# One more pair's softmax denominators on VectorE, and multiplies and token sums on GpSimd, in a two-layer convolution and attention kernel

## The chip, the cores and the metric

The kernel runs on one core of one Trainium2 chip, as one launch. The metric is the device time of one execution in microseconds (us). A core has TensorE (PE, matrix products into PSUM), VectorE (DVE), ScalarE (ACT), GpSimd (POOL) and SyncE (SP), each with an instruction stream of its own, taken in order; SP here issues the DMAs. All data are float32.

## The reference

Eight images of 768 channels and 32 x 32 = 1024 tokens go through two layers, each of which adds to its input:

```python
x = x + attention(group_norm(x))          # layer 0
x = x + correlation_conv(group_norm(x))   # layer 1

def attention(x):                          # 12 heads of 64
    q, k, v = split(x_flat @ W_qkv.T)
    var_v, var_k = var(v, axis=-1, ddof=1), var(k, axis=-1, ddof=1)   # one number per token
    attn = softmax(var_v @ var_k.T * 64 ** -0.5)
    return (attn @ v) @ W_proj.T + b_proj

def correlation_conv(f):
    n = f / max(norm(f, axis=channels), 1e-12)
    corr = [sum(shifted(n, r, c) * n, axis=channels) for r, c in 28 offsets]
    return conv_w @ concat(f, corr) + conv_b                          # 1 x 1
```

The scores are an outer product of two vectors, so that no score matrix product is needed: an exponential of one row, scaled per partition, gives a block of the softmax's numerator.

## The kernel before, in words

**Products.** The three large products (keys and values, projection, convolution) are made by a scheme of seven block products in place of eight; it needs sums of operand blocks (`TokenSums`, L1030, for projection and convolution; `make_sums`, L595, on GpSimd for keys and values) and adds the seven results up in PSUM banks x, y and z (`Banks`, L340 on; both halves of a product are issued by `halves`, L333 to L337). A unit is one such block product: 1.93 us by the plan for keys and values, 2.58 for the wide ones. After a unit, VectorE (in part ScalarE) takes the bank to SBUF. The next unit that adds to that bank waits for this. The token sums are t1, t2, a third that is written over the input, and t4, three instructions of 128x512 each; their names in the profile end in f for the convolution, in o for the projection.

**Attention.** An image has six pairs of heads. For a pair, `exponentials` (L733) makes on ScalarE two tiles ex of 128x1024 for each of eight steps; `products` (L757) multiplies them with the values on TensorE (av, L763). Four steps are run together. The denominators are had in one of two ways, by the table `SUMMED` (L47):

- a pair not in it makes them on ScalarE: `denominators` (L742), 16 further exponentials junk from the tiles bk, then an inverse on VectorE (invs), a transpose on TensorE (it, in `spread`, L870) and a DMA through memory (di) that spreads it over partitions as rd;
- a pair in it adds its ex tiles up on VectorE (acc, L775), 14 additions; then `sum_up` (L790) sums over the partitions by four matmuls of 32 columns (den, L797), ScalarE copies, and DMAs bring the sums to a narrow tile inv for the reciprocal and back as rd. The image's last pair (`sum_up_last`, L840) instead makes wide sums by L847 and four reciprocals of 128x256 (`invert`, L853), with no DMA.

`finish` (L885) multiplies the pair's result (tile v) by the inverses. The acc tiles and the bk tiles share two buffers; rd has one. Image 0 sums pairs 0, 3, 4 and 5; the others 3, 4 and 5.

**Correlation.** `Corr` (L1069) multiplies blocks of the normalised image, turned by GpSimd (turn, L1086), with the image (gr, L1101), takes windows (win) out through DRAM, and scales them (dd, m, rn on GpSimd in L1146, dn); `to_dram` transposes dn on TensorE (ct, L340) and a DMA gathers rows cs. The convolution adds cs by short products (L1008) to its banks.

**Order.** No engine is told when to start; the program's order is computed while it is built, with a model clock (`Clock`, L79). `later.after(us, job)` issues a job when the model clock has moved on by us; `after_dve` counts from the end of VectorE's modelled work; `ready` holds keys of what has been issued, and `act_work` queues ScalarE's. `work_off` chooses between four attention steps, a correlation product beside it and the next unit of the rest: the second half of keys and values, then the previous image's convolution. Then `project` makes the projection, and the next image's first half of keys and values follows. On the chip each engine takes its instructions in that order and waits by semaphores for data and buffers.

**Start.** Image 0 is loaded and its group norm made; meanwhile 36 products of the identity with itself run on TensorE (warm, L390). `Norm.means` and `Norm.spreads` (L476, L487) then put two small products on TensorE, pm and pv; GpSimd makes the power rstd, and the image is scaled (xn). L153 is the line of a helper through which every VectorE instruction goes, L215 that of ScalarE's copies.

Of the kernel before, what the change touches and what calls it, by code (L numbers as in the profile page):

```python
# [13 lines left out]
P = 128  # L14
# [32 lines left out]
SUMMED = ((0, 3, 4, 5), (3, 4, 5))  # L47
# [7 lines left out]
WARM = 36  # L55
# [103 lines left out]
def two_layers(ctx, tc, x, wkv, wproj, bproj, wconv, wcorr, bconv, out):  # L159
# [308 lines left out]
    class Norm:  # L468
# [239 lines left out]
    class Pair:  # L708
# [131 lines left out]
        def sum_up_last(self):  # L840
# [189 lines left out]
    class TokenSums:  # L1030


        def __init__(self, name, low, high, third=None):
            self.low, self.high = low, high
            self.name = name
            self.third = third or [a[:, HF:] for a in low]
# [4 lines left out]
        def first(self):  # L1041
            self.t1 = self.place(1)
            for k in range(JH):
                a = self.low[k]
                vector.tensor_tensor(self.t1[:, k, :], a[:, HF:], a[:, :HF], ALU.subtract)

        def second(self):
            self.t2 = self.place(2)
            for k in range(JH):
                vector.tensor_tensor(self.t2[:, k, :], self.high[k][:, HF:], self.t1[:, k, :], ALU.subtract)  # L1050

        def thirds(self):
            for k in range(JH):
                vector.tensor_tensor(self.third[k], self.high[k][:, HF:], self.low[k][:, HF:], ALU.subtract)

        def fourth(self):
            self.t4 = self.place(4)
            for k in range(JH):
                vector.tensor_tensor(self.t4[:, k, :], self.high[k][:, :HF], self.t2[:, k, :], ALU.subtract)
# [9 lines left out]
    class Corr:  # L1069
# [70 lines left out]
        def scale(self, hf, dd):  # L1140
# [7 lines left out]
            def columns():  # L1148
# [4 lines left out]
                later.after_dve(0.7, lambda: to_dram(dn))  # L1153
# [46 lines left out]
    class Conv:  # L1200


        def __init__(self, b, f, acc, after):
# [4 lines left out]
            self.sums = TokenSums(f"f{b}", [f[:, k, :] for k in range(JH)], [f[:, JH + k, :] for k in range(JH)])  # L1208
# [124 lines left out]
    def project(b, ots, held=None):  # L1333
# [35 lines left out]
        sums = TokenSums(f"o{b}", ots[:JH], ots[JH:])  # L1369
# [166 lines left out]
```

## Time and profile before

| What | Value |
|---|---|
| median of 3 runs | 2643.72 us (2642.43 to 2647.05) |
| the profiled execution, its own time | 2640.38 us |
| its span | 2638.7 us |
| granted TensorE clock, mean | 0.998 |
| ScalarE denominators (junk, L748) | 368, mean 1143 ns |
| what ends each (read of the sum) | 368, mean 187 ns |
| VectorE additions acc<-acc,ex and acc<-ex,ex | 300 of 1209 ns and 50 of 1215 ns |
| VectorE multiplies v<-v,rd and v<-v,acc | 40 of 1211 ns and 8 of 1223 ns |
| VectorE token sums (t1f, f, t2f, t4f; the o ones alike) | 128x512, 663 to 687 ns |
| GpSimd sums s, 128x384 | 256, 1003 to 1098 ns by line |
| rd loads from di, from den | 46, 34 of 256 KB |

In the profile an engine's row gives its busy time and its share of the span. Groups of instructions show the line, the engine, the operation, what is written and read (out<-in, buffer numbers left out), the shape and the count. The waits name who waited for whom, in us in total, times and the longest. The timeline gives start, duration, engine, line and operation, and in brackets the idle time of the engine in front of it with what ended it. A product of a whole tile is two records on TensorE; both halves of a unit run beside one another. Images are counted from 0; attention of image 3 runs from about 1003 us to 1192, its projection from about 1207.

### The profile page before, as it was taken

What the parts mean: (1) busy time and instruction counts of PE and PEld (TensorE: products, weight loads), DVE (VectorE), ACT (ScalarE), POOL (GpSimd) and SP (SyncE); (2) the same over time, 40 slices, a digit from 0 to 9 for tenths busy, and PEclk for the clock granted to TensorE, in tenths of its full rate; (3) what the DMA queues carried; (4) which work ended last, traced back from release to release, by engine and by line L of the source; (5) the groups of instructions that cost most, each with busy time, mean ns of one, the idle gap of its engine ahead of it and who ended that gap; (6) DMA issues with size and microseconds to landing.
All of it is one profiled execution on the core that took longest, in us unless ns stands there. A gap on an engine that the chain in (4) does not pass through costs nothing.

```text
span 2638.7 us, 40466 instructions
## 1 busy us (share of the span) xinstructions
PE 2610.0 (99%) x14766; PEld 1318.2 (50%) x14766; DVE 1604.3 (61%) x4110; ACT 1367.3 (52%) x1841; POOL 413.6 (16%) x444
## 2 busy tenths in 40 slices
PE   9999999999999999999999999999999999999999
PEld 4654566334763347633476334553357433575333
DVE  5858735685447853478534885357853587535864
ACT  1498078711598116980179701897018960199500
POOL 4320130003300033000430003300133001320000
PEclk9999999999999999999999999999999999999999
DMA  7774455455553545626556265562655626545333
GB/s 285 291 247 147 144 198 158 137 182 159 188 187 113 201 153 180 198 95 214 155 172 196 87 220 158 171 205 81 221 172 154 196 84 237 169 137 164 96 117 101
DMA packets 323392, 446.65 MB, mean 169 GB/s; under 512 B 59458, under 2 KB 245170, under 8 KB 323194
## 3 DMA queue, kind: packets, MB, share of 16 engines
q1 hardware_dynamic: 321962, 441.32, 52.0%
q8 instruction: 117, 1.92, 0.3%
q10 hardware_dynamic: 1232, 2.75, 0.3%
q14 instruction: 81, 0.66, 0.1%
HBM read 377.49 MB, written 64.40 MB: 167 GB/s over the span
## 4 chain that ended last, share of the span: by engine, by line
PE 89%; DMA 3%; ACT 3%; DVE 2%; issue 1%; SPq 1%; POOL 1%; DVEq 0%; ACTq 0%; POOLq 0%
PE x L337 35%; PE av L763 22%; PE y L337 17%; PE z L337 9%; PE gr L1101 3%; ACT ex L738 1%; ACT junk L748 1%; DMA x<-x1d 1%; DMA v<-rows 1%; DMA bc<-vdr 1%; PE x L1008 1%; PE den L797 1%; PE y L1008 1%; PE z L1008 1%; DVE acc L153 1%
## 5 line engine op out<-in xcount | busy, mean ns | idle before, releaser
L738 ACT ACTIVATE ex<-bc,nk 128x1024 f32<-128x1024 f32 x768 | 828.2, 1138 | 418.7 <-DMA bc<-vdr 202.6
L763 PE MATMUL av<-ex,v 128*64 128x512 f32 x3072 | 700.2, 596 | 3.4 <-ACT ex L738 3.2
L763 PEld LDWEIGHTS av<-ex,v 128*64 128x64 f32 x3072 | 316.6, 137 | 339.0 <-issue 210.5
L748 ACT ACTIVATE junk<-bk,vm 128x1024 bf16<-128x1024 f32 x368 | 420.5, 1143 | 25.3 <-DMA bk<-kdr 15.5
L153 DVE TENSOR_TENSOR acc<-acc,ex 128x1024 f32<-128x1024 f32 x300 | 344.3, 1209 | 0.0
L215 ACT COPY kp<-x 128x384 f32<-128x384 f32 x28 | 13.4, 477 | 562.1 <-PE x L337 553.4
L337 PE MATMUL y<-kv,s 128*64 128x384 f32 x1488 | 269.4, 487 | 0.0
L337 PE MATMUL x<-kv,xn 128*64 128x384 f32 x1512 | 264.3, 489 | 1.6 <-DVE xn L153 1.6
L337 PE MATMUL x<-kv,s 128*64 128x384 f32 x1488 | 258.2, 486 | 0.0
L337 PEld LDWEIGHTS x<-kv,xn 128*64 128x64 f32 x1512 | 145.3, 138 | 101.1 <-issue 80.5
L337 PEld LDWEIGHTS x<-kv,s 128*64 128x64 f32 x1488 | 145.2, 137 | 91.2 <-issue 67.6
L337 PEld LDWEIGHTS y<-kv,s 128*64 128x64 f32 x1488 | 140.7, 137 | 87.1 <-issue 69.2
L494 POOL TENSOR_TENSOR rstda<-vea,neghalf 128x1 f32<-128x1 f32 x8 | 4.8, 595 | 964.4 <-DVE vea L153 964.4
L1086 POOL TENSOR_TENSOR turn<-f,ones 128x384 f32<-128x384 f32 x112 | 110.9, 1010 | 248.3 <-PE gr L1101 167.6
L337 PE MATMUL z<-kv,xn 128*64 128x384 f32 x768 | 135.1, 486 | 0.0
L337 PE MATMUL x<-v,wt 128*64 128x512 f32 x576 | 131.1, 594 | 0.0
L337 PE MATMUL x<-f,wt 128*64 128x512 f32 x504 | 120.1, 594 | 0.0
L153 DVE TENSOR_TENSOR v<-y,v 128x128 f32<-128x128 f32 x180 | 40.9, 282 | 127.3 <-PE y L337 127.3
L600 POOL TENSOR_TENSOR s<-xn 128x384 f32<-128x384 f32 x64 | 66.8, 1052 | 287.2 <-PE x L337 199.0
L153 DVE BATCH_NORM_STATS2 vbn<-v 128x6 f32<-128x64 f32 x720 | 101.6, 209 | 0.0
L337 PEld LDWEIGHTS z<-kv,xn 128*64 128x64 f32 x768 | 76.4, 137 | 45.9 <-issue 34.3
L1101 PEld LDWEIGHTS gr<-f,turn 128*64 128x64 f32 x1344 | 88.3, 137 | 13.2 <-issue 5.2
(192 smaller groups left out, 3006.5 us busy)
## 6 DMA issues: line engine op xcount, KB each, us to landing
kv<-kvs SPq DMA_DIRECT2D x124, 576.0 KB
kv<-in_wkv_dram SPq DMA_DIRECT2D x95, 576.0 KB
bc<-vdr SPq DMA_DIRECT2D x96, 512.0 KB
f<-in_x_dram SPq DMA_DIRECT2D x48, 512.0 KB
bk<-kdr SPq DMA_DIRECT2D x46, 512.0 KB
x1d<-f SPq DMA_DIRECT2D x42, 512.0 KB
x<-x1d SPq DMA_DIRECT2D x42, 512.0 KB
out_dram<-x SPq DMA_DIRECT2D x82, 256.0 KB
```

The costliest lines, as they stand in the source:

```text
L153: return getattr(self.engine, name)(*args, **kw)
L215: nc.scalar.copy(to, at)
L337: nc.tensor.matmul(out[at], lhsT=lhsT[:, at], rhs=rhs, start=start, stop=stop, **kw)
L494: nc.gpsimd.tensor_tensor(self.rstd, ve, neghalf[:, 0:1], ALU.pow)
L600: nc.gpsimd.tensor_tensor(self.sums[g][:, 0], a[g][2], a[g][3], ALU.add)
L738: nc.scalar.activation(ex, self.bc[e], AF.Exp, scale=self.kv.nk[self.half][:, h, t : t + 1])
L748: nc.scalar.activation(junk, self.bk[e], AF.Exp, scale=self.kv.m2[self.half][:, h, t : t + 1], accum_out=self.sums[:, e, t : t + 1],)
L763: nc.tensor.matmul(self.av[e * HD : (e + 1) * HD, hf, :], lhsT=self.vt[:, t, e, :], rhs=exs[e][:, hf * HF : (hf + 1) * HF], start=t == 0, ...
L797: nc.tensor.matmul(den[at * 32 : (at + 1) * 32, :], lhsT=ones[:, 0:32], rhs=self.acc[e][:, hf * HF : (hf + 1) * HF], start=True, stop=True,)
L1008: nc.tensor.matmul(t, lhsT=wcorr_sb[at, i, :], rhs=cs[at, tokens, :], start=False, stop=True, skip_group_check=True)
L1086: nc.gpsimd.tensor_tensor(to[:, :, side], half, windows(ones, ones.ap[0], (0, J), (HW, 4), (1, HW)), ALU.mult)
L1101: nc.tensor.matmul(ps[side * HD : (side + 1) * HD, :n].rearrange("p (y x) -> p y x", x=WIDE), lhsT=block[:, j, side, :], rhs=image[:, 4 * ...
```

## The change

- Pair 0 is summed in all images, no longer in image 0 alone.
- `finish` multiplies on GpSimd for pairs 0 to 4 and on VectorE for pair 5; a pair on GpSimd counts as ready 2.5 us of model time later.
- The convolution's token sums go to GpSimd in images 0 to 6 and stay on VectorE in image 7; the projection's stay on VectorE. `TokenSums` takes the engine as an argument, in place of one that no call used.
- In images 1 to 7 the last pair's first reciprocal is issued 2.6 us of model time after its sums, which was 1.2, and the following ones 1.0 us after VectorE's modelled work, which was 1.5.
- In image 0's correlation, `to_dram` is issued 3.0 us after VectorE's modelled work, which was 0.7.
- 42 warm products in place of 36, and 6 and 12 more of them behind image 0's two small products of the first group norm. The tile that they write to is of the pool of av, not of the pool of small products.

```diff
-SUMMED = ((0, 3, 4, 5), (3, 4, 5))
+SUMMED = ((0, 3, 4, 5), (0, 3, 4, 5))
...
-WARM = 36
+WARM, BRIDGE = 42, (6, 12)
...
-    warm = smp.tile([P, 512], F32, tag="sm", name="warm")
-    for n in range(WARM):
-        nc.tensor.matmul(warm[:, 0:P], lhsT=ident, rhs=ident, start=True, stop=True)
+    warm = avp.tile([P, 512], F32, tag="av", name="warm")
+
+    def keep_warm(count):
+        for n in range(count):
+            nc.tensor.matmul(warm[:, 0:P], lhsT=ident, rhs=ident, start=True, stop=True)
+
+    keep_warm(WARM)
...
             halves(pm[:, 0:1], group_m, mv[:, 0:1])
+            if name == "a0":
+                keep_warm(BRIDGE[0])
...
             halves(pv[:, 0:1], group_m, self.e)
+            if name == "a0":
+                keep_warm(BRIDGE[1])
...
-                    later.after_dve(1.5 if self.b else 0.0, lambda: invert(n + 1))
+                    later.after_dve(1.0 if self.b else 0.0, lambda: invert(n + 1))
...
-            later.after(1.2 if self.b else 0.0, lambda: invert(0))
+            later.after(2.6 if self.b else 0.0, lambda: invert(0))
...
         def finish(self):
-            vector.tensor_tensor(self.ot, self.ot, self.rd, ALU.mult)
+            last = self.hp == HP - 1
+            (vector if last else nc.gpsimd).tensor_tensor(self.ot, self.ot, self.rd, ALU.mult)
             self.finished = True
             self.bk_free = True
-            ready.add(("ot", self.b, self.hp))
+            later.after(0.0 if last else 2.5, lambda: ready.add(("ot", self.b, self.hp)))
...
-        def __init__(self, name, low, high, third=None):
+        def __init__(self, name, low, high, engine):
+            self.engine = engine
...
-                vector.tensor_tensor(self.t1[:, k, :], a[:, HF:], a[:, :HF], ALU.subtract)
+                self.engine.tensor_tensor(self.t1[:, k, :], a[:, HF:], a[:, :HF], ALU.subtract)
...
-                vector.tensor_tensor(self.t2[:, k, :], self.high[k][:, HF:], self.t1[:, k, :], ALU.subtract)
+                self.engine.tensor_tensor(self.t2[:, k, :], self.high[k][:, HF:], self.t1[:, k, :], ALU.subtract)
...
-                later.after_dve(0.7, lambda: to_dram(dn))
+                later.after_dve(0.7 if b else 3.0, lambda: to_dram(dn))
...
-            self.sums = TokenSums(f"f{b}", [f[:, k, :] for k in range(JH)], [f[:, JH + k, :] for k in range(JH)])
+            self.sums = TokenSums(f"f{b}", [f[:, k, :] for k in range(JH)], [f[:, JH + k, :] for k in range(JH)], nc.gpsimd if b < NB - 1 else vector)
...
-        sums = TokenSums(f"o{b}", ots[:JH], ots[JH:])
+        sums = TokenSums(f"o{b}", ots[:JH], ots[JH:], vector)
```

The third and fourth sums change in the same way as the first two.

More of the change, by code (lines that the diff above doesn't have):

```diff
@@ L1030, in two_layers @@
     class TokenSums:
-        def __init__(self, name, low, high, third=None):
+        def __init__(self, name, low, high, engine):
+            self.engine = engine
             self.low, self.high = low, high
             self.name = name
-            self.third = third or [a[:, HF:] for a in low]
+            self.third = [a[:, HF:] for a in low]
         def place(self, n):
@@ L1049, in second @@
             for k in range(JH):
-                vector.tensor_tensor(self.t2[:, k, :], self.high[k][:, HF:], self.t1[:, k, :], ALU.subtract)
+                self.engine.tensor_tensor(self.t2[:, k, :], self.high[k][:, HF:], self.t1[:, k, :], ALU.subtract)
         def thirds(self):
             for k in range(JH):
-                vector.tensor_tensor(self.third[k], self.high[k][:, HF:], self.low[k][:, HF:], ALU.subtract)
+                self.engine.tensor_tensor(self.third[k], self.high[k][:, HF:], self.low[k][:, HF:], ALU.subtract)
         def fourth(self):
@@ L1058, in fourth @@
             for k in range(JH):
-                vector.tensor_tensor(self.t4[:, k, :], self.high[k][:, :HF], self.t2[:, k, :], ALU.subtract)
+                self.engine.tensor_tensor(self.t4[:, k, :], self.high[k][:, :HF], self.t2[:, k, :], ALU.subtract)
         def operand(self, p, k):
```

## The prediction

> **What bounds the kernel now.** The page comes first, its busy shares:
>
> ```profile
> PE 2610.0 (99%) x14766; PEld 1318.2 (50%) x14766; DVE 1604.3 (61%) x4110; ACT 1367.3 (52%) x1841; POOL 413.6 (16%) x444
> ```
>
> TensorE is the bound in every stage: 2638.7 us of span less 2610.0 busy leaves 28.7 us. So no other engine's average matters; only two things move the end: work put on or taken off TensorE, and its few waits. The waits of TensorE, longest first (total us, times, longest), name them:
>
> ```profile
> PE x L337 <- DVE x L153: 4.6, 6, 0.9
> PE ct L340 <- DVE dn L153: 3.3, 1, 3.3
> PE av L763 <- ACT ex L738: 3.2, 2, 2.4
> PE ptv L340 <- DVE vm L153: 2.3, 3, 1.2
> ...
> PE x L337 <- DVE xn L153: 1.6, 1, 1.6
> PE x L337 <- DVE t2o L153: 1.6, 1, 1.6
> ```
>
> The timeline then shows where each sits. The six waits of the first row come once in each of images 2 to 7, at the convolution's end. VectorE there, and TensorE's instruction that waits:
>
> ```profile
> 875.43 1.76 DVE L153 RECIPROCAL acc<-den 128x256 f32<-128x256 f32 x1 [4.18 <-PE den L847]
> 877.10 1.16 DVE L153 TENSOR_TENSOR v<-v,rd 128x1024 f32<-128x1024 f32 x1
> 878.18 0.68 DVE L153 TENSOR_TENSOR x<-z,x 128x512 f32<-128x512 f32 x1
> 878.77 0.68 DVE L153 TENSOR_TENSOR x<-x,x 128x512 f32<-128x512 f32 x1
> ```
> ```profile
> 879.51 2.79 PE L337 MATMUL x<-t4f,wt 128*64 128x512 f32 x12 [0.72 <-DVE x L153]
> ```
>
> The bank x had been full since about 874.3; VectorE emptied it only after a reciprocal and a multiply. The ct wait is single, in image 1 at 392 to 396 us, and the pair-3 wait in image 1 at 475 to 478 us. TensorE, then GpSimd (rn, which ct's data wait for), then TensorE again:
>
> ```profile
> 395.70 0.44 PE L340 MATMUL ct<-ident,dn 128*64 128x128 f32 x4 [3.33 <-DVE dn L153]
> 395.94 3.37 PE L763 MATMUL av<-ex,v 128*64 128x512 f32 x8
> ```
> ```profile
> 393.71 1.02 POOL L1146 TENSOR_TENSOR rn<-m,neghalf 128x4 f32<-128x4 f32 x1
> ```
> ```profile
> 477.70 3.86 PE L763 MATMUL av<-ex,v 128*64 128x512 f32 x7 [2.45 <-ACT ex L738]
> ```
>
> Such matmuls elsewhere start every 0.215 us (32 of them in 6.87 us of the chain), so 8 in 3.37 and 7 in 3.86 us are slow: each wait is followed by about 1.7 to 2.3 us lost. The same at the start, where 24 records take 5.79 us and the next 24 start 3.87 us apart:
>
> ```profile
> 16.87 5.79 PE L337 MATMUL x<-kv,xn 128*64 128x384 f32 x24 [1.63 <-DVE xn L153]
> 22.49 4.04 PE L337 MATMUL z<-kv,xn 128*64 128x384 f32 x24
> ```
>
> [...] The trace agrees that they disturb each other, not that one fully blocks: GpSimd's s sums take 1.00 us in the median and up to 2.53 beside VectorE's weight sums, which rise from 1.36 to at most 2.15.
>
> **The change part by part.**
>
> *Pair 0 in images 1 to 7.* Off ScalarE go 7 x 16 denominators of 1.143 + 0.187 us, 149 us; on VectorE come 7 x 14 additions of 1.21, 119 us. Neither is on TensorE's path in images 2 to 7. On TensorE, a transpose (it, 2 records from 1062.33 to 1062.55, 0.22 us) gives way to four 32-column matmuls of sum_up:
>
> ```profile
> 850.61 1.06 PE L797 MATMUL den<-acc,ones 128*32 128x512 f32 x8
> 851.61 4.94 PE L763 MATMUL av<-ex,v 128*64 128x512 f32 x22
> ```
>
> That is 1.00 us from start to start, and the y product in front ends 0.10 late (it started at 847.93 and needs 2.57). Net 1.10 - 0.22 = 0.88 us, in 7 images **+6.2 us**, on the path and certain. Do the additions make TensorE wait for its banks? Image 0 already runs pair 0 this way beside the same half of keys and values: from 96 to 150 us the timeline shows no TensorE wait. I take 0; upper bound 1 us an image, 7. On SP two 512 KB bk loads and a di store go, four den stores, an inv load and an inverse store come: some 3 issues more, about 1 us of SP an image. No TensorE wait is released by these transfers; 0. Pair 1's bk loads now wait for pair 0's sum_up matmuls; ScalarE's denominators of pair 1 start later, but it has 21 us an image in hand.
>
> *Pair 3 in image 1.* ScalarE still had pair 2's denominators between pair 3's exponentials. With 21 us fewer ahead of it this goes: 2.45 + (3.86 - 7 x 0.215 = 2.3, of which I count 1.75) = **-4.2**. Bounds 0 (bc's landing at 463 us becomes what is late) and -4.7. Next late there: bc.
>
> *ct of image 0's correlation.* It is issued 2.3 us later, with other matmuls ahead of it: the wait falls from 3.3 to 1.0[...]: -2.3 - (3.37 - 1.72) = **-4.0**. Bounds 0 and -5.0. VectorE's own 7.2 us wait for rn stays.
>
> *Reciprocals.* The first comes 2.6 instead of 1.2 us after the matmuls of the last pair, the next ones 1.0 instead of 1.5 apart: the two evacuations of x go ahead, TensorE has nothing to wait for: **-4.6**. The chain's end moves by 1.4 - 3 x 0.5 = -0.1 us, so t2o, which is next and in image 2 is in time by about 0.1 us, isn't later. Bounds: -5.5, and 0 if the wait moves to t2o.
>
> *Multiplies on GpSimd.* 40 of 1.211 us leave VectorE. [...] Only the last pair's product is due soon, and that stays on VectorE. What it waits for is rd: VectorE waited 75.7 us in 14 such instructions, up to 10.7. This wait now stands in GpSimd's queue, ahead of turn (TensorE's gr waits for it), the s sums (its kv products), rn and most (VectorE's dn and nk). Pair 1's long one came at 1106 to 1117, with no work of GpSimd till 1130: I take 0; bounds -2.3 (the ptv waits, since VectorE is free) and +2 us an image, 14.
>
> *Token sums on GpSimd, images 0 to 6.* 84 of 0.68 us leave VectorE, 84 of 1.27 come. t1f is made four kv units (8 us) before its use; t2f is issued 3.5 us after the convolution's start. In image 3 it would start after most (1092.0), end at 1095.8 in quiet and at 1100.8 at the 2.3-fold of the disturbed s; TensorE reads it at 1102.56. Cover: the 6.9 us of four attention steps that lie between. I take 0; without that cover TensorE would come at 1095.7, and the wait is 0.1 to 5.1 us an image.
>
> *Start.* 6 more warm matmuls (0.224 each by the last records' spacing) end before 13.88: 0. The 6 behind pma hold pva 0.4 us; the 12 behind pva, 2.7 us, end near 18.2, past the data. So products start 1.3 later but at full clock: 1.3 - 1.9 = **-0.6**; bounds -1.9 and +1.3.
>
> *The 2.5 us before a pair counts as finished and the warm tile's other pool* move issue order alone: 0, hidden by units that need neither.
>
> Sum: +6.2 - 4.2 - 4.0 - 4.6 - 0.6 = **-7.2**. From the profiled execution's 2640.38 that is 2633.2. It is 3.34 under the median of the runs, so by the median 2643.72 - 7.2 = **2636.5 us**.
>
> **Rivals.**
> *More goes than I count* (0.20): VectorE no longer held by rd; ptv (2.3), the t2o wait (1.6), the rest of the start (1.3) and den's wait for acc (1.0) go too: 2630.3. For it: all these wait for VectorE. Against: at 1415 ptv was late by a wait for x1d, which stays.
> *Waits move on* (0.19): the x wait turns up at t2o and pair 3's at bc; 8.8 us aren't gained: 2645.3. For it: t2o's 0.1 us of margin, and bc landing at 463 us. Against: VectorE loses a 1.16 us multiply there. If ct's stays too, the change is just its TensorE cost, 2649.3.
> *GpSimd's t2f is late* (0.15): attention is now ahead and its four steps fall elsewhere; 7 images wait the middle of 0.1 and 5.1, 2.6 us: -7.2 + 18.2 = +11.0, 2654.7, **slower**. It decides from 1.0 us an image, and passes +0.2% at 1.8. For it: sums on GpSimd are twice as long and share SBUF with additions. Against: pace of image 3.
> Unnamed waits, about 2650: 0.06. Forecast: 0.40.
>
> **How the numbers follow.** 0.2% is 5.3 us, about what a measurement here can tell from no change: below 2638.4 lie most of the forecast (0.36) and the first rival (0.19), 0.55; above 2649.0 half of the last parts of moving waits (0.05), t2f (0.14) and unnamed (0.06), 0.25; between, 0.20. Range 2627 to 2655: below it 0.06 of the first rival's tail, above it 0.08 of t2f's. Both signs hold chance; the forecast's own range is 2632 to 2641.
>
> **What would show it.** L797's den from 136 to 192 records and it from 46 to 32; TensorE's wait for x gone and that for t2o no longer than 1.6 us; ct under 1.2 us and no slow burst after it; first product near 18.2 with 24 records in about 4 us. Wrong if t2f or turn of GpSimd appear among TensorE's waits over 5 us in total, or busy TensorE grows by more than 8 us.

## The result, and the profile after

| Kernel | Median, us | Ratio to before, 95% interval |
|---|---|---|
| before | 2643.07 (2641.60 to 2647.05, 4 runs) | 1 |
| changed | 2693.18 (2689.71 to 2694.42, 4 runs) | 1.0185 (1.0172 to 1.0197) |

The change makes the kernel 49 us slower. The profiled execution took 2693.62 us, its span 2691.5. Lines of the changed kernel stand 8 to 10 higher (av L771, ex L746, junk L756, den L805, gr L1111). First the busy shares on its page:

```profile
PE 2638.8 (98%) x14856; PEld 1283.4 (48%) x14856; DVE 1686.6 (63%) x4077; ACT 1243.7 (46%) x1624; POOL 652.5 (24%) x568
```

TensorE still bounds it: its busy time grew by 28.8 us and its idle time (span less busy) from 28.7 to 52.7. Its granted clock is not the cause, with a mean of 0.999 in all four runs against 0.998 before. Work was moved off ScalarE as meant (1367 to 1244), and none of that shows in the time. TensorE's waits (total us, times, longest):

```profile
PE av L771 <- ACT ex L746: 22.4, 14, 2.8
PE ct L340 <- DVE dn L153: 7.9, 6, 1.3
PE x L337 <- DVE f L153: 5.5, 6, 0.9
PE gr L1111 <- POOL turn L1096: 4.7, 10, 1.5
...
PE x L337 <- DVE t2o L153: 1.6, 1, 1.6
```

The 4.6 us for x at the convolution's end and ptv's 2.3 are gone. In their place TensorE waits 22.4 us for exponentials (3.2 before), 7.9 for dn (3.3, once) and 4.7 for turn. The third row is new. It stands in front of a product of t2o in six images, not where the projection starts (1226.87 in image 3) but near its end, where the next image's group norm begins. TensorE makes pva, a small product of that norm, one unit later than before (in image 3 it stood in front of y<-t1o, at 1245.73). VectorE's vea reads pva and waits 3.33 us for it, where it waited 0.76 before; behind vea in VectorE's queue stands the instruction that empties bank x. TensorE, then VectorE:

```profile
1268.24 0.23 PE L337 MATMUL pva<-ea,group 128*64 128x1 f32 x4
1269.39 2.80 PE L337 MATMUL x<-t2o,wt 128*64 128x512 f32 x12 [0.92 <-DVE f L153]
```
```profile
1268.52 0.16 DVE L153 TENSOR_SCALAR vea<-pva 128x1 f32<-128x1 f32 x1 [3.33 <-PE pva L337]
1268.59 0.74 DVE L153 SCALAR_TENSOR_TENSOR f<-x,bproj_sb,f 128x512 f32<-128x512 f32 x1
```

Of the places that the prediction named, the two in image 1 came out as it said. The ct matmuls wait no longer, and 31 products of pair 3 run with nothing in between:

```profile
399.15 0.27 PE L340 MATMUL ct<-ident,dn 128*64 128x128 f32 x1
...
468.54 7.67 PE L771 MATMUL av<-ex,v 128*64 128x512 f32 x31
```

At the start, warm products fill the gaps and the first 24 products run at full speed: 4.09 us, with a granted clock of 1.00 from 18.79 to 22.70, where before they took 5.79, with 0.70 from 16.87 to 22.50. But they begin 1.9 us later than before (18.79 against 16.87), and z begins at 22.71 against 22.49:

```profile
15.92 2.94 PE L392 MATMUL warm<-ident 128*128 128x128 f32 x24
18.79 4.09 PE L337 MATMUL x<-kv,xn 128*64 128x384 f32 x24
22.71 4.04 PE L337 MATMUL z<-kv,xn 128*64 128x384 f32 x24
```

The loss recurs in each of images 2 to 7. From the first t2o product of one image's projection to that of the next it is 332.6 to 336.4 us up to image 6, and 323.6 to 324.9 before; to image 7's it is 325.0 against 318.1. In image 3 three places show it.

**Pair 1's first steps.** ScalarE copies ds, then stands still for 5.5 us in front of a denominator of pair 1. The profile puts this down to a DMA, though not to the right one (rows<-cr); the denominator reads bk, whose loads SP issued from 1055.59 on, and by the program that tile is what it needs. Three exponentials stand behind it in ScalarE's queue:

```profile
1053.75 0.58 ACT L215 COPY ds<-den 128x512 f32<-128x512 f32 x1 [1.35 <-PE den L805]
1059.85 1.15 ACT L756 ACTIVATE junk<-bk,vm 128x1024 bf16<-128x1024 f32 x1 [5.51 <-DMA rows<-cr]
...
1061.00 3.21 ACT L746 ACTIVATE ex<-bc,nk 128x1024 f32<-128x1024 f32 x3
```
```profile
1062.18 2.54 PE L771 MATMUL av<-ex,v 128*64 128x512 f32 x7 [1.62 <-ACT ex L746]
```

TensorE gets its exponentials 1.62 us late. The seven matmuls behind that take 2.54 us, by an estimate some 0.7 us more than at the usual 0.215 us from start to start, though the clock granted from 1062 to 1066 us was full (1.00).

**dn and ct.** GpSimd's multiply and its three t1f run just while VectorE makes dn. GpSimd first, then VectorE, then TensorE:

```profile
1076.50 1.02 POOL L1156 TENSOR_TENSOR rn<-m,neghalf 128x4 f32<-128x4 f32 x1 [11.52 <-DVE m L153]
1077.49 2.37 POOL L895 TENSOR_TENSOR v<-v,rd 128x1024 f32<-128x1024 f32 x1
1079.83 3.73 POOL L1055 TENSOR_TENSOR t1f<-f 128x512 f32<-128x512 f32 x3
```
```profile
1077.55 2.34 DVE L153 COPY dn<-rn 128x4 f32<-128x4 f32 x1 [1.13 <-POOL rn L1156]
1079.80 3.94 DVE L153 SCALAR_TENSOR_TENSOR dn<-dd,rn,mask 128x19 f32<-128x19 f32 x4
```
```profile
1083.80 0.44 PE L340 MATMUL ct<-ident,dn 128*64 128x128 f32 x4 [1.31 <-DVE dn L153]
```

A copy of four elements a line (0.166 us before) takes 2.34 us and ends when GpSimd's multiply ends (1079.89 and 1079.86); the four small multiplies behind it (0.232 each) take 3.94 beside the three t1f, and both end within 0.2 us of each other.

**The start of pair 3.** ScalarE has four denominators of pair 2 between pair 3's exponentials, and VectorE's first addition of pair 3 takes 3.30 us beside t4f on GpSimd (1132.38 to 1136.14). VectorE, then TensorE:

```profile
1133.92 3.30 DVE L153 TENSOR_TENSOR acc<-ex,ex 128x1024 f32<-128x1024 f32 x1
```
```profile
1142.56 2.54 PE L771 MATMUL av<-ex,v 128*64 128x512 f32 x7 [1.63 <-ACT ex L746]
```

The order of ScalarE's queue is enough for this wait: e13 below has it too, with the addition at its usual length.

### The profile page after: what moved, and what is told of

Read it like the earlier page. It is cut to its first block, busy times and chain, and to the rows that moved or that the text cites. A ratio compares the mean times of both kernels' runs of the same rounds, so it can differ in the third digit from the quotient of the medians.

```text
span 2691.5 us, 40831 instructions
## 1 busy us (share of the span) xinstructions
PE 2638.8 (98%) x14856; PEld 1283.4 (48%) x14856; DVE 1686.6 (63%) x4077; ACT 1243.7 (46%) x1624; POOL 652.5 (24%) x568
## 4 chain that ended last, share of the span: by engine, by line
PE 84%; DMA 5%; issue 3%; ACT 3%; DVE 3%; POOL 3%; SPq 0%; POOLq 0%; ACTq 0%; DVEq 0%
PE x L337 33%; PE av L771 20%; PE y L337 16%; PE z L337 9%; PE gr L1111 3%; ACT ex L746 2%; DMA vdr<-rsv 2%; DMA bc<-vdr 1%; POOL turn L1096 1%; ACT junk L756 1%; DVE dn L153 1%; PE den L805 1%; PE x L1017 1%; PE y L1017 1%; PE den L855 1%
## 5 line engine op out<-in xcount | busy, mean ns | idle before, releaser
L746 ACT ACTIVATE ex<-bc,nk 128x1024 f32<-128x1024 f32 x768 | 825.9, 1138 | 504.7 <-DMA bc<-vdr 245.2
L771 PE MATMUL av<-ex,v 128*64 128x512 f32 x3072 | 715.6, 596 | 23.5 <-ACT ex L746 22.4
L771 PEld LDWEIGHTS av<-ex,v 128*64 128x64 f32 x3072 | 308.3, 137 | 376.8 <-issue 221.3
L153 DVE TENSOR_TENSOR acc<-acc,ex 128x1024 f32<-128x1024 f32 x384 | 456.5, 1248 | 4.0 <-ACT ex L746 4.0
L756 ACT ACTIVATE junk<-bk,vm 128x1024 bf16<-128x1024 f32 x256 | 292.6, 1143 | 47.9 <-DMA bk<-kdr 28.7
L895 POOL TENSOR_TENSOR v<-v,rd 128x1024 f32<-128x1024 f32 x40 | 107.9, 2699 | 526.0 <-DMA rd<-den 297.1
L337 PEld LDWEIGHTS x<-kv,xn 128*64 128x64 f32 x1512 | 133.8, 137 | 111.7 <-issue 94.2
L337 PEld LDWEIGHTS x<-kv,s 128*64 128x64 f32 x1488 | 136.6, 137 | 99.2 <-issue 83.2
L1096 POOL TENSOR_TENSOR turn<-f,ones 128x384 f32<-128x384 f32 x112 | 131.0, 1190 | 193.5 <-PE gr L1111 139.3
L608 POOL TENSOR_TENSOR s<-xn 128x384 f32<-128x384 f32 x64 | 67.3, 1062 | 270.1 <-PE x L337 179.3
L153 DVE SCALAR_TENSOR_TENSOR x<-x,bconv_sb,x 128x512 f32<-128x512 f32 x63 | 46.5, 748 | 112.1 <-PE x L337 67.9
L153 DVE TENSOR_TENSOR acc<-ex,ex 128x1024 f32<-128x1024 f32 x64 | 95.4, 1522 | 31.2 <-ACT junk L756 29.9
```

What stands on the lines that cost most here:

```text
L153: return getattr(self.engine, name)(*args, **kw)
L337: nc.tensor.matmul(out[at], lhsT=lhsT[:, at], rhs=rhs, start=start, stop=stop, **kw)
L608: nc.gpsimd.tensor_tensor(self.sums[g][:, 0], a[g][2], a[g][3], ALU.add)
L746: nc.scalar.activation(ex, self.bc[e], AF.Exp, scale=self.kv.nk[self.half][:, h, t : t + 1])
L756: nc.scalar.activation(junk, self.bk[e], AF.Exp, scale=self.kv.m2[self.half][:, h, t : t + 1], accum_out=self.sums[:, e, t : t + 1],)
L771: nc.tensor.matmul(self.av[e * HD : (e + 1) * HD, hf, :], lhsT=self.vt[:, t, e, :], rhs=exs[e][:, hf * HF : (hf + 1) * HF], start=t == 0, ...
```

## The experiments

Two theories stood at first. **B**: pair 0's sums hold the buffers that pair 1's bk tiles need, and ScalarE, in order, stands in front of them. **G**: GpSimd's new instructions lengthen VectorE's. A third, **O**, was formed on the way: the program order itself has moved. Every kernel computes all of the reference. Each was timed in five rounds beside the kernel before, whose median in the five sets of runs was 2639.15 to 2642.26 us; so ratios are compared, and "difference" is (ratio - 1) x 2642. A difference between two of these runs is known to some 3 to 6 us. The "small changes" are the reciprocals' times, ct's time in image 0 and the warm products at the start.

| Run | What it is | Median, us | Ratio (interval) | Difference |
|---|---|---|---|---|
| e4 | pair 0 alone | 2665.91 | 1.0088 (1.0075 to 1.0102) | +23 |
| e5 | e4, denominators queued when due | 2640.42 | 1.0003 (0.9995 to 1.0011) | +1 |
| e1 | pair 0 and small changes | 2663.32 | 1.0081 (1.0068 to 1.0093) | +21 |
| e13 | changed kernel's order, VectorE executes | 2680.06 | 1.0145 (1.0127 to 1.0163) | +38 |
| changed | order moved, GpSimd executes | 2693.18 | 1.0185 (1.0172 to 1.0197) | +49 |
| e14 | e1's order, GpSimd executes | 2700.91 | 1.0221 (1.0201 to 1.0241) | +58 |
| e6 | changed, pair 0's multiply on VectorE | 2680.57 | 1.0156 (1.0142 to 1.0170) | +41 |
| e7 | changed, pair 2 summed for pair 0 | 2726.05 | 1.0328 (1.0313 to 1.0342) | +87 |
| e9 | changed, denominators when due | 2680.44 | 1.0156 (1.0140 to 1.0173) | +41 |
| e11 | e5 and small changes | 2645.96 | 1.0026 (1.0017 to 1.0035) | +7 |
| e12 | e11, multiplies on GpSimd | 2686.80 | 1.0181 (1.0165 to 1.0196) | +48 |
| e15 | e5's order, multiplies executed by GpSimd | 2639.07 | 0.9991 (0.9984 to 0.9997) | -2 |
| e17 | e15 with the start | 2639.31 | 0.9989 (0.9981 to 0.9997) | -3 |
| e3 | small changes alone | 2646.72 | 1.0017 (1.0010 to 1.0025) | +4 |
| e8 | e3, token sums on GpSimd | 2647.82 | 1.0030 (1.0018 to 1.0042) | +8 |
| e2 | e3, both moves to GpSimd | 2631.72 | 0.9963 (0.9949 to 0.9976) | -10 |
| e10 | e3, multiplies on GpSimd | 2630.91 | 0.9967 (0.9955 to 0.9979) | -9 |
| e16 | e10, reciprocals at old times | 2632.00 | 0.9962 (0.9949 to 0.9975) | -10 |
| e18 | e3's order, multiplies executed by GpSimd | 2630.55 | 0.9964 (0.9951 to 0.9976) | -10 |

### Which part costs: e1 to e4

e1, from the changed kernel (the ready time too goes back):

```diff
-            (vector if last else nc.gpsimd).tensor_tensor(self.ot, self.ot, self.rd, ALU.mult)
+            vector.tensor_tensor(self.ot, self.ot, self.rd, ALU.mult)
...
-            self.sums = TokenSums(f"f{b}", ..., nc.gpsimd if b < NB - 1 else vector)
+            self.sums = TokenSums(f"f{b}", ..., vector)
```

> The changed kernel with finish and the convolution's token sums on VectorE again; pair 0 stays summed, the small order changes stay. Theory G (GpSimd's new instructions lengthen VectorE's and turn, and ct, gr and av wait for that): about 2653 us, the dn copy back to 0.17 us, ct no longer among TensorE's waits, and what stays is pair 0's TensorE cost (6) and ScalarE's wait for bk (some 2 us an image, 12), less the gains of the small changes (9). Theory P (pair 0 as sums is what costs, GpSimd nothing): 2690, no change against the changed kernel. The prediction's own sum: 2636.

e2, from the changed kernel; e3 has e1's and e2's edits together:

```diff
-SUMMED = ((0, 3, 4, 5), (0, 3, 4, 5))
+SUMMED = ((0, 3, 4, 5), (3, 4, 5))
```

> The changed kernel with the old table, pair 0 on ScalarE in images 1 to 7; multiplies and token sums stay on GpSimd. Theory G: about 2672 us (2693 less 6 for den and 14 for the bk wait in front of pair 1); ct still waits for dn. Theory P: 2640. A third theory, that the two only hurt together (VectorE with 14 more additions an image has no room left for longer instructions): about 2645 here and about 2645 with GpSimd's work back on VectorE.

> The changed kernel with all three large parts undone: only the reciprocals' times, ct's time in image 0 and the warm products at the start stay. The prediction's working gives -4.6 -4.0 -0.6 = -9.2 against before: 2634 us. If the wait for x only moves to t2o, as the trace of the changed kernel suggests (0.9 us an image): about 2638. If the ct wait in image 1 stays as well: 2642.

e4, from the kernel before, is the same line the other way round.

> The kernel before with pair 0 summed in all images and nothing else. By the prediction's terms for pair 0 and for pair 3 in image 1: +6.2 -4.2 = +2.0, 2645 us. With ScalarE's wait for bk in front of pair 1 in each image (Theory B, 2.2 us an image as in the changed kernel): 2659 us, and TensorE's wait av for ex shows six times near the first steps of pair 1.

Measured: 2663, 2632, 2647 and 2666. Pair 0 alone costs 23 us, as Theory B had it (2659 and more), with nine waits for ex, 11.9 us in all. In e4 the waits for x, for ct and for pair 3 in image 1 are gone, and ptv's but for 0.3 us, although it has none of the small changes; the wait for t2o is there in five images (4.6 us). So pair 0 alone takes what the small changes were to gain. By the ratios GpSimd's part is a gain of 14 us when pair 0 stays on ScalarE (e3 to e2), and a loss of 27 when it doesn't (e1 to the changed kernel): neither G nor P, and nearest to the third theory, though that one had pair 0 harmless by itself.

e3 was the surprise. The small changes are a loss by themselves (interval +3 to +7 us): TensorE's wait for x rose from 4.6 to 9.9 us and that for ptv from 2.3 to 7.0, while ct's fell from 3.3 to 1.3. VectorE and TensorE at the end of image 3's convolution:

```profile
1199.57 1.23 DVE L153 TENSOR_TENSOR v<-v,rd 128x1024 f32<-128x1024 f32 x1 [5.55 <-DMA rd<-den]
1200.71 1.75 DVE L153 RECIPROCAL acc<-den 128x256 f32<-128x256 f32 x1
1202.38 0.63 DVE L153 TENSOR_TENSOR x<-z,x 128x512 f32<-128x512 f32 x1
1202.93 0.68 DVE L153 TENSOR_TENSOR x<-x,x 128x512 f32<-128x512 f32 x1
```
```profile
1203.66 2.79 PE L337 MATMUL x<-t4f,wt 128*64 128x512 f32 x12 [2.09 <-DVE x L153]
```

The later reciprocal no longer stands in front of pair 4's multiply. So VectorE reaches the multiply first and waits 5.55 us there for rd; reciprocal and evacuations come after it.

### Theory B: e5

From e4; only the order in which ScalarE's work is queued changes:

```diff
             else:
-                clock.act_work(
-                    SUM, lambda: pair.rows_at.get(("k", e)), lambda: self.denominators(pair, t, e), 1
-                )
+                def due():
+                    at = pair.rows_at.get(("k", e))
+                    late = self.b and pair.hp == 1 and at is not None and at > clock.now + 0.5
+                    return None if late else at
+
+                clock.act_work(SUM, due, lambda: self.denominators(pair, t, e), 1)
```

> The kernel before with pair 0 summed in all images, and ScalarE's denominators of pair 1 not queued before the plan has their tiles bk landed (images 1 to 7), so that pair 1's next exponentials go in front of them. Against pair 0 alone (2666 us): if ScalarE's wait for bk, in front of exponentials that TensorE needs, is what costs (Theory B), TensorE's waits for ex fall from 11.9 us to below 4, the slow matmuls behind them go too, and the time is about 2650; 6 us of TensorE's den and the waits for turn are left. If ScalarE has no room there anyhow and the wait comes back a few steps later: 2660 or more.

Measured: 2640.42, below what was expected. The waits for ex fall from 11.9 to 1.8 us. ScalarE at the same place as in the first fences:

```profile
1038.14 0.58 ACT L215 COPY ds<-den 128x512 f32<-128x512 f32 x1 [1.36 <-PE den L797]
1041.37 4.27 ACT L738 ACTIVATE ex<-bc,nk 128x1024 f32<-128x1024 f32 x4 [2.64 <-PE av L763]
1045.54 1.13 ACT L748 ACTIVATE junk<-bk,vm 128x1024 bf16<-128x1024 f32 x1
```

Four exponentials go ahead, and the first denominator finds its tile there. The early place came from the plan: with exponentials held back by their buffers, it took the only other job, a denominator, and let its clock run on to the time at which bk would land. On the chip everything queued behind it waited as long (in e4's image 3 ScalarE stood idle for 5.49 us in front of that denominator, and four exponentials came behind it). TensorE's den costs and the waits for turn (4.4 us) are still in e5; they are made good by the waits for x, for ct, for ptv and for pair 3 in image 1 that went. Not all of e5's gain over e4 is ScalarE's queue: the wait for t2o (4.6 us) went too, since pva is back in its old place.

### Theory G, and other places for the work: e6, e7, e8

e6 and e7 from the changed kernel, e8 from e3 with the token sums on GpSimd:

```diff
-            (vector if last else nc.gpsimd).tensor_tensor(self.ot, self.ot, self.rd, ALU.mult)
+            (vector if last or (self.hp == 0 and self.b) else nc.gpsimd).tensor_tensor(self.ot, self.ot, self.rd, ALU.mult)
```

> The changed kernel with one multiply moved back to VectorE, that of pair 0 in images 1 to 7; the other 33 stay on GpSimd. Theory G: pair 0's multiply on GpSimd runs beside VectorE's dn and stretches it (0.17 to 2.3 us), and TensorE's ct waits for that: the ct wait (7.9 us in total) and the slow matmuls behind it go, 2680 to 2684 us. If t1f alone stretches dn as much: ct keeps more than half of its wait, 2688 to 2692. If GpSimd has nothing to do with ct (VectorE is late by its additions): 2693.

```diff
-SUMMED = ((0, 3, 4, 5), (0, 3, 4, 5))
+SUMMED = ((0, 3, 4, 5), (2, 3, 4, 5))
```

> The changed kernel with pair 2 summed in images 1 to 7 in place of pair 0, so that no pair with tiles bk follows a summed one within an image; TensorE and VectorE have exactly as much work as in the changed kernel. If what costs is where pair 0's additions and its bk wait lie: TensorE's 6 us on top of the kernel with pair 0 back on ScalarE (2632), with some 5 us for new collisions: 2638 to 2645. If VectorE's load as such costs (14 more additions an image beside GpSimd's longer instructions): 2685 to 2695.

> The small order changes and the convolution's token sums on GpSimd, nothing else (pair 0 on ScalarE, multiplies on VectorE). Between the small changes alone (2646.7) and both moves to GpSimd (2631.7). If the token sums on GpSimd are what makes x's evacuation in time at the convolution's end: x's 9.9 us of waiting go and the time is 2637; if the multiplies are (VectorE no longer held up by rd): nothing changes, 2646, and the waits for ptv stay.

e6: 2680.57, as Theory G said, 8 us less than the changed kernel by the ratios (12.6 by the medians, which are of different sets of runs). ScalarE and SP have exactly the changed kernel's order here, and TensorE's as far as its trace shows. So a single multiply an image, on GpSimd, made ct late; its wait falls from 7.9 to 0.3 us. e8: 2647.82, so the token sums on GpSimd are no gain; the waits for ptv went, but seven for ct came (7.6 us) and x's stayed (9.5). e7 missed by far: 2726. Its trace shows what can meet there. VectorE's six nk (0.90 us for the six in e12, 0.88 in the changed kernel) beside GpSimd's t2f, first VectorE, then GpSimd:

```profile
1114.51 6.29 DVE L153 TENSOR_SCALAR nk<-km,most 128x8 f32<-128x8 f32 x6
1120.71 4.62 DVE L153 TENSOR_TENSOR acc<-acc,ex 128x1024 f32<-128x1024 f32 x4
```
```profile
1113.57 4.62 POOL L1060 TENSOR_TENSOR t2f<-f,t1f 128x512 f32<-128x512 f32 x3 [9.12 <-issue]
1118.15 8.32 POOL L1064 TENSOR_TENSOR f<-f 128x512 f32<-128x512 f32 x3
```

The additions come late, ScalarE waits for them since they hold the ex buffers, and TensorE for ScalarE (35.1 us in 13 waits, 12.7 more than in the changed kernel). TensorE also waits 10.0 us for additions in front of den, and once 4.8 for t2f. How much of the 38 us between e7 and the changed kernel (by the ratios) is the disturbance and how much is order wasn't told apart.

### Does the loss stay when B is mended: e9 to e12

e9 is the changed kernel with e5's edit, e10 is e3 with multiplies on GpSimd, e11 is e1 with e5's edit, e12 is e11 with multiplies on GpSimd and their ready time.

> The whole change, with ScalarE's denominators of pair 1 not queued before their tiles bk have landed in the plan, as in the kernel of before with pair 0 (there it took 25 us off). Theory B says that at least those 25 us go here as well, 2668 or less; if the late exponentials of pair 1 are also what makes GpSimd's moves harmful beside pair 0 (they cost 30 us there and gained 15 without it), more goes: about 2640. If GpSimd's moves cost by themselves as soon as VectorE has pair 0's additions (ct stays at 8 us, pair 3's av wait at about 10): 2665 to 2670.

> The small order changes and the multiplies on GpSimd, nothing else (pair 0 on ScalarE, token sums on VectorE). Token sums alone gained nothing (2647.8 against 2646.7), both moves together 15 us. If the multiplies are the part that gains, since VectorE is then not held up by rd: the waits for ptv and x of the small changes alone (17 us) go, 2631 or, with fewer disturbed dn than with both moves, 2628. If it needs both: 2640 or more.

> Pair 0 summed and the small changes, denominators of pair 1 queued when due, nothing on GpSimd. The same without the small changes gave 2640.4; the start gained 3 us with pair 0 before, so 2637 if the reciprocals' and ct's times are harmless here, 2640 or more if the later reciprocals delay t2o or x again as they do without pair 0.

> As the last one, with the multiplies on GpSimd as in the change (token sums on VectorE). The two gains would add if they don't meet: 2637 less some of the 15 us that GpSimd's moves gained without pair 0, at most the 2 to 4 us of waits that are still there: 2633 to 2636. If pair 0's multiply beside VectorE's dn makes ct wait again (Theory G, 6 images of about 2 us with the slow matmuls behind): 2648.

e10 gave 2630.91: the multiplies are the part that gains. e11 gave 2645.96, worse than e5 by 0.0023 in the ratio: with the small changes the wait in front of t2o is back, five times (4.6 us). e9 (2680) and e12 (2687) missed. In both the waits for ex are gone, and six waits for invs, at the change from pair 2 to 3, have come in their place (21.5 and 28.5 us). In e12's image 3, SP, VectorE and TensorE:

```profile
1117.09 1.75 SPq L735 DMA_DIRECT2D bc<-vdr  x4
1118.89 1.28 SPq L1227 DMA_DIRECT2D x<-x1d  x1
```
```profile
1128.55 0.75 DVE L153 SCALAR_TENSOR_TENSOR x<-y,bconv_sb,x 128x512 f32<-128x512 f32 x1 [6.89 <-DMA x<-x1d]
1129.22 0.24 DVE L153 RECIPROCAL invs<-sums 128x16 f32<-128x16 f32 x1
```
```profile
1129.52 0.48 PE L340 MATMUL it<-ident,invs 128*64 128x128 f32 x1 [4.79 <-DVE invs L153]
```

In e11, where VectorE waits at most 3.2 us for such a load, SP issued the fourth x1d before the four loads of bc:

```profile
1106.14 0.41 SPq L1227 DMA_DIRECT2D x<-x1d  x1
1110.52 1.75 SPq L735 DMA_DIRECT2D bc<-vdr  x4
```

So the program order had moved on SP although only multiplies had changed engine. The plan counts VectorE's instructions in its clock and not GpSimd's; what is issued by after_dve comes earlier once they leave it. That the four large loads in front are what made x1d late is read from the order alone.

### Order or engine: e13 to e18

e13 keeps the changed kernel's order on TensorE, ScalarE and SyncE line for line, and only the engine is VectorE (nc.vector is called past the plan's clock). e14 is the converse, e1's order with GpSimd executing, counted as if it were VectorE. e15 is e5 with counted multiplies.

```diff
-            (vector if last else nc.gpsimd).tensor_tensor(self.ot, self.ot, self.rd, ALU.mult)
+            (vector if last else nc.vector).tensor_tensor(self.ot, self.ot, self.rd, ALU.mult)
```
```diff
-    vector = Vector(nc.vector, clock)
+    vector, counted = Vector(nc.vector, clock), Vector(nc.gpsimd, clock)
...
-            vector.tensor_tensor(self.ot, self.ot, self.rd, ALU.mult)
+            (vector if last else counted).tensor_tensor(self.ot, self.ot, self.rd, ALU.mult)
```

(The token sums in e13 and e14 alike.)

> The changed kernel with its program order kept exactly on TensorE, ScalarE and SyncE, but multiplies and token sums executed by VectorE, without their being counted in the plan's clock. The kernel with them on VectorE and counted took 2663, the changed one 2693. Theory O (the order: on GpSimd they leave the plan's VectorE clock, and what is issued after VectorE's modelled work moves): 2690 or more, since the order is the same. Theory G (GpSimd's slow instructions and their disturbance of VectorE): about 2663, and dn's copy is 0.17 us again and ct no longer waited for. A mixture of both would lie between, by the share of each.

> The converse: the order of the kernel with pair 0 and the small changes (2663), kept exactly on TensorE, ScalarE and SyncE, but multiplies and token sums executed by GpSimd, counted in the plan's clock as if VectorE made them. Theory O: 2663 or a few us less. Theory G: 2690.

> Pair 0 on VectorE with denominators of pair 1 queued when due (2640.4, next to no waits), with its order kept exactly, and the multiplies of pairs 0 to 4 executed by GpSimd. Multiplies moved the plain way took 41 us here (2646 to 2687), with TensorE waiting for it behind VectorE's wait for x1d. Theory O: 2638 to 2642. Theory G: 2665 or more, with TensorE waiting for ct or it.

> Multiplies on GpSimd, ct's time in image 0 and the start, with pair 0 on ScalarE, token sums on VectorE and the reciprocals at their old times. With the new times it took 2630.9, and small changes alone 2646.7 in place of the expected 2634. If the later reciprocals are what made the small changes fail (x waited 2.2 us for VectorE in place of 0.9): 2626 here. If they are worth the 4.6 us of the prediction: 2635.

e13: +38, between the two: order alone takes the +21 of e1 to +38, and the engine takes that to +49. With VectorE executing, ct isn't waited for at all, and the waits for ex stay:

```profile
PE av L771 <- ACT ex L746: 22.1, 14, 2.2
PE x L337 <- DVE f L153: 5.5, 6, 0.9
```

Their places tell where the order costs. In images 2 to 7 e1 has them at pair 1 only; e13 and the changed kernel have six more at the start of pair 3, one in each of these images, 10.6 us in e13. In image 3 of e13 VectorE's first addition of pair 3 takes its usual 1.22 us, so GpSimd isn't needed for this wait. What e13 shares with the changed kernel is ScalarE's queue, which stands idle for 3.68 us in front of pair 3's first exponentials (3.95 in the changed kernel) and has four denominators between them; e1 has no such gap, and one denominator. VectorE, then TensorE in e13:

```profile
1127.85 1.22 DVE L153 TENSOR_TENSOR acc<-ex,ex 128x1024 f32<-128x1024 f32 x1
```
```profile
1136.24 2.54 PE L771 MATMUL av<-ex,v 128*64 128x512 f32 x7 [1.39 <-ACT ex L746]
```

e14 shows that in the old order the engine alone costs even more, 37 us. There the rival that the prediction named does happen, t2f from GpSimd comes late, once by 13.1 us in image 1 and then by 1 to 2 us in each of images 2 to 7, beside the same ct waits; the waits for ex are those of e1 (11.7):

```profile
PE x L337 <- POOL t2f L153: 20.8, 19, 13.1
PE av L771 <- ACT ex L746: 11.9, 10, 1.6
PE ct L340 <- DVE dn L153: 7.9, 6, 1.3
```

GpSimd, where t2f is late in image 1:

```profile
458.98 0.40 POOL L685 PARTITION_ALL_REDUCE most<-top  x1 [6.26 <-DMA x<-x1d]
472.48 3.71 POOL L153 TENSOR_TENSOR t2f<-f,t1f 128x512 f32<-128x512 f32 x3 [13.10 <-issue]
```

The profile names nothing that t2f waits for, but what stands in front of it in GpSimd's queue is most. In the traces of the kernel before and of the changed one there are 32 of these, and GpSimd never starts its next instruction earlier than 6.67 us after one (6.95 in the kernel before). Behind its other instructions it often starts the next at once, as t1f behind the multiply in the fence above on dn and ct. If the 6.67 us are a fixed price, which no run here tests, they are half of the 13.1. In images 2 to 7 GpSimd stands idle in front of t2f for 10.1 us in the mean (73.9 in all seven, less the 13.1).

e15: 2639.07. In this order GpSimd's multiplies, 2.88 us each in the mean, hurt nobody. So the 41 us of e11 to e12 were most likely order; e12's own order with VectorE executing was not run. e15 moves no token sums, and so doesn't contradict e14. e16: 2632.00, the same as e10 within the intervals: once the multiplies are on GpSimd, the reciprocals' times don't matter.

> Pair 0 summed, pair 1's denominators queued when due, multiplies executed by GpSimd in an order that counts them (2639.1 so far), with the change's warm products at the start. These were worth 3 us with pair 0 (2666 to 2663, together with the other small changes): 2636. If the start changes nothing once the other waits are gone: 2639.

> The small changes with pair 0 on ScalarE, in their order (2646.7) kept exactly on TensorE, ScalarE and SyncE, but the multiplies of pairs 0 to 4 executed by GpSimd and counted as before. Left uncounted they gave 2630.9, 16 us less. If that gain is VectorE no longer being held up by rd in front of ptv's inputs and of x: 2631 here too, and TensorE's waits for x and ptv are gone. If it came from the order that moved: 2645, and these waits stay.

e17 is e15 with the change's warm products, e18 is e3 with counted multiplies and so with e3's order. e18 took 2630.55: the gain isn't order but VectorE's relief. VectorE at the place shown for e3:

```profile
1196.29 1.76 DVE L153 RECIPROCAL acc<-den 128x256 f32<-128x256 f32 x1 [4.18 <-PE den L855]
1197.96 0.63 DVE L153 TENSOR_TENSOR x<-z,x 128x512 f32<-128x512 f32 x1
1198.51 0.68 DVE L153 TENSOR_TENSOR x<-x,x 128x512 f32<-128x512 f32 x1
```

No multiply stands between, TensorE waits for x no more, and for ptv 2.6 in place of 7.0 us. e17, 2639.31, is the best version with pair 0 summed; the start adds nothing that can be measured (0.9991 to 0.9989).

**What beats both kernels**: multiplies of pairs 0 to 4 on GpSimd with pair 0 left on ScalarE (e10, e16, e18; the token sums make no difference, e2), 9 to 10 us or 0.35% below before.

## Why the prediction was wrong, point by point

Forecast 2636.5, measured 2693.2; outside the range, and the other side. By differences in ratio the 49 us are, taken in this sequence: pair 0 alone +23 (e4), small changes with it -2 (e1, no more than the noise), the order that the moves to GpSimd bring +17 (e13), GpSimd executing +11 (the changed kernel). Each is known to some 4 to 6 us either way, and the parts depend on the sequence: with e1's order the engine takes 37 us (e14).

- **Pair 0, +6.2: the step that failed most.** The records went as said (den L805 to 192, it to 32). What failed is the sentence on pair 1's bk loads, "ScalarE's denominators of pair 1 start later, but it has 21 us an image in hand". The wait was seen, and an average was put against it. ScalarE takes its queue in order, and behind the denominator that waited 5.51 us stood exponentials due at once. e5 takes 22 us off, most of it by letting these go first. In the changed kernel the same edit took only 8 us off (e9), as waits for invs came in the place of those for ex.
- **Multiplies on GpSimd, 0: failed, twice.** On GpSimd a multiply took 2.37 us undisturbed, against 1.211 on VectorE before. Without pair 0 they are a gain of 14 us (e3 to e18), since VectorE isn't held up by rd (5.55 us at the place shown for e3); the text saw VectorE wait 75.7 us for rd and gave up to 2.3 for it. (The rival "more goes than I count" had this, and e10 meets its 2630.3 with 2630.91, but with pair 0 left out; the number is luck.) In the change they bring a loss, since the 0 left out the program order: GpSimd isn't in the plan's clock. "The 2.5 us before a pair counts as finished ... move issue order alone: 0" took order for harmless, and here order costs 17 us, with pair 3's six waits for exponentials as its main visible part.
- **Token sums, 0: the size held, the cover was looked for in the wrong place.** Each took 1.27 to 1.37 us in the mean; the prediction's 1.27 was not shown by the trace before. In the changed kernel TensorE doesn't wait for t2f. But t1f, and pair 0's multiply ahead of it, cover dn on VectorE, and ct waits. Only queues were searched for who waits, not who is on VectorE at that time. The working also let t2f start right after most (1092.0). With the 6.67 us that at least lie behind most in the two kernels' traces it would end at about 1102.9 (an estimate: 1092.0, 0.44 for most itself, 6.67 and 3.8), with TensorE reading it at 1102.56, so that none of the cover is left. The rival's mechanism appears in e14.
- **Disturbance.** The prediction read the trace as "not that one fully blocks". The changed kernel says otherwise: dn's copy lasted as long as the multiply beside it (2.34 us against 2.37) and ended 0.03 us after it, and so it went in six images. What holds the one while the other runs was not shown.
- **Reciprocals, -4.6: failed.** In e3, the small changes without pair 0, the wait for x grew by 5.3 us. The sum counted VectorE's instructions in front of x and not that the multiply, now first, would stand waiting for rd. In the changed kernel the wait for x is gone, but it is gone in e4 and e16 too, with the reciprocals at their old times, so the gain isn't theirs. The rival "waits move on" named t2o, and 5.5 us of waiting for a t2o did come; but it came at the other end of the projection, from pva's place in the order, and e4 has it with the old reciprocals. The rival was right on the name only, by luck.
- **Pair 3 in image 1, -4.2, and ct of image 0's correlation, -4.0: right where they were predicted**, as the lines of image 1 show. But ct's was counted as a gain of its own, and pair 0 alone removes it (e4); without pair 0 the later time left 1.3 us (e3), where 1.0 was forecast. The same two waits then opened in images 2 to 7. The slow matmuls that the prediction counted behind these waits came with a lower granted clock in the kernel before: 0.58 behind ct's 3.33 us (395.7 to 399.1) and 0.56 behind pair 3's 2.45 (477.7 to 481.6), but 1.00 behind the 0.72 in front of x (879.5 to 882.3). In the changed kernel the clock fell behind two waits only, of 2.13 and 1.96 us (0.62 from 726.5 to 731 us, 0.66 from 808 to 813), and not behind one of 2.62 (1.00 from 1476 to 1481).
- **Start, -0.6: nothing.** First product at 18.79, not 18.2; z begins 0.2 later.
- **What was to show it wrong did**: TensorE's busy time grew by 28.8 us against the 8 given. e5, with pair 0's matmuls and next to no new waits, has 8.3 us more than before; so some 20 of the 28.8 come with the waits (an estimate). turn stayed just below its mark of 5 (4.7).

What stays open: how the 38 us of e7 divide, what t2f waited for in e14's image 1 beyond the 6.67 us behind most, how much e14 owes to its token sums and how much to its multiplies, and how much of order's 17 us is the ready time of 2.5 us and how much the plan's clock, since both were changed together.

## What to carry to other kernels

An engine's idle time on average is no cover for one instruction that waits: look at what stands behind it in the same queue, and whether it can be queued later (one condition took off 22 us). Where a planner's clock sets the order, work moved to an engine that the clock doesn't count moves everything else as well; time the move with the order kept, and the order with the engine kept, before believing either. Move to GpSimd what waits for a slow transfer and is due late (here the multiplies, 14 us gained without pair 0), and keep it away from times at which short VectorE instructions feed TensorE (here dn, 7.9 us of waiting).

## What had not been expected of the hardware

Beside a GpSimd instruction on SBUF, some small VectorE instructions lasted until their neighbour ended. In the changed kernel dn's copy of four elements a line went from 0.166 to between 2.34 and 2.35 us in six images, and ended 0.03 us after GpSimd's multiply each time; in the same images three of the four multiplies of 19 elements went from 0.232 to between 1.30 and 1.33 (beside t1f of 1.26 to 1.29 each), and each ended within 0.04 us of the end of a t1f. In e7 six nk went from 0.90 to 6.29. A larger one, an addition, went from 1.22 to 3.30 and ended 1.09 us after t4f. These read two tiles of SBUF, or copy or scale one from SBUF to SBUF. Not all suffer: in the changed kernel the statistics vbn<-v (0.21 us), x<-x,bconv_sb,x, which reads PSUM and SBUF (0.75), and the reciprocal inv<-inv (0.24 to 0.25) took as long beside GpSimd as without it. Long additions suffer little in the mean: in the changed kernel acc<-acc,ex took 1.248 us against 1.209, though a pair's first, acc<-ex,ex, took 1.522 against 1.215. GpSimd's instructions grow as well: its multiplies, 2.37 us undisturbed, took up to 5.13. In the changed kernel it is VectorE's short instructions on the way to TensorE that show in its waits, 7.9 us for dn.

The second is GpSimd's own: after most, a PARTITION_ALL_REDUCE (0.40 us in the line of e14), it never started anything sooner than 6.67 us later, in the 32 cases of the two kernels' traces. No run tests why; but here work that is due soon, as t2f is, should not stand behind it.
